# Four graph layers in one kernel: q's bias moved into ScalarE copies, two small products with 64-column weights, and another precomputed order

## The chip, the cores and the metric

The kernel runs on one core of one Trainium2 chip. A core has five engines that run their own instruction queues in order: TensorE (PE in the profile, its weight loads PEld), VectorE (DVE), ScalarE (ACT), GpSimd (POOL) and SyncE (SP), which here issues the DMAs. They wait for each other through semaphores. The metric is the device time of one execution in microseconds (us), taken as the median of several runs; lower is better. One execution was also recorded by the hardware profiler, and its trace is what the views below are read from.

## The reference, cut to what matters

Input x is 128 graphs of 64 nodes with 512 features, adj is 128 matrices of 64 x 64. Four layers follow each other, each of the form x + f(relu(layernorm(x)), adj):

```python
# layer 0: hypergraph convolution twice, H = (adj != 0), w = first row of adj
xw  = h @ W1.T                               # 512 -> 1024
m   = Be * (H.T @ xw);  out = Dn * (H @ m) + b1
z   = layer_norm(relu(out), gamma, beta)
y   = the same convolution of z with W2, b2  # 1024 -> 512
# layer 1: attention from two sums, s = (h @ w) @ a
A   = exp(lrelu(8 * tanh((s_i + s_j) / 8), 0.1)) * adj
out = (A / A.sum(-1) * adj.sum(-1)) @ h @ w
# layer 2: attention with q, k, v
q, k, v = h @ Wq.T + bq, h @ Wk.T + bk, h @ Wv.T + bv
wt  = adj * exp(q @ k.T);  out = (wt / wt.sum(2)) @ v
# layer 3: three-hop diffusion
T   = adj * exp(lrelu(sj + si + ab, 0.2)), rows normalised
out = relu(h @ Wk[0] + bk[0] + T h @ Wk[1] + bk[1] + T T h @ Wk[2] + bk[2])
```

## The kernel before, in words

Tokens are the 128 x 64 nodes; a tile is 128 tokens (two graphs), a group is 4 tiles, and there are 16 groups. A first stage takes every group through layers 0 and 1 and writes x to DRAM (L819); a second stage takes every group through layers 2 and 3 (the loops at the end of the kernel function). Weights stay in SBUF; W1, W2 and w of the first stage are replaced by those of the second. All matmuls are fp32, and each runs as two passes on TensorE, so the trace shows two records for each.

Large products are done with a seven-product scheme over 2 x 2 blocks (`strassen`, L600, for layers 0, 1 and 3; `prod` of layer 2, L851). The common tail is `seven` (L573): three PSUM buffers px, py and pz take the seven products; after four of them ScalarE copies the running sum out into SBUF (`snap`, L581, the copy is L582), and `emit` finishes one of the four output blocks: block (0,0) from py plus the first snapshot, (1,1) from two snapshots, (0,1) from pz plus a snapshot, (1,0) from px. `emit` differs by layer: `biased` (L640) adds a bias row to the snapshot on GpSimd (L646) and the product on VectorE (L648), giving y; `emit_q` (L866) adds q's bias to the snapshot on GpSimd (L876) and the product on VectorE (L877). Block (1,0) has no snapshot, and there ScalarE adds the bias as it copies (L870).

Small products around the change:
- M (L716): per group, four tiles of H^T times (B^-1 H, first column of adj) in one PSUM buffer, 128 columns of weights by 65 moving columns; then two copies of the diagonal blocks (L719). M multiplies h (`left_mul_T`, L547) and finally y (L769).
- T^2 (L968): per group, four tiles of T with T's transpose, 128 by 64; the transposes are VectorE's (L959). T and T^2 multiply h at L984.
- The logits of layer 2 (L889): 32 matmuls with weights of 128 rows by 64 columns, for the two halves of PSUM's partitions in turn.
- L922 multiplies the attention weights with v, which `emit_v` finishes at L912.

The attention sums of layers 1 and 3 need a column of sums spread over all partitions: `across` (L650) writes it to DRAM (L656) and reads it back twice as a row (L660), on SP's queue. Layer 1's rows' denominator (L794) goes the same way. `load_group` (L337) loads a group's adjacency (L339) and x tiles (L345); L790 is the first user of the adjacency in layer 1, L705 to L711 in layer 0.

The order of everything is computed when the kernel is built. Each operation is recorded with an engine, a price in us, and the buffers it reads and writes (`Graph.op`); nothing is issued then. `Graph.run` (L82) plays the operations in time with these prices and with fixed latencies: among those that can start first on an engine it takes the one of lowest priority number, gives out buffers as they come free, and notes the order. The priority of an operation is a running time (`G.prio`), advanced by `step(us)` times STRETCH for the layer and set to group x PERIOD1 or PERIOD2 at each group, plus a shift for the part of the layer it belongs to (`part`, which looks the shift up in the table AT). The instructions are then emitted in that order. Each engine keeps it on the chip, whatever the durations really are.

Where `run` finds TensorE idle for more than 0.5 us, `fill` (L1020) puts matmuls of ones in front of the next product, so many that they take 0.75 of the gap that was computed:

```python
for _ in range(int(gap * FILL / (0.224 if filled else 0.448))):
    nc.tensor.matmul(ps[:, :P], ones, ones, start=True, stop=True)
```

A planned wait thus becomes visible in the code as a number of filler matmuls (L1024), 89 in all in the kernel before.

Of the kernel before, what the change touches and what calls it, by code (L numbers as in the profile page):

```python
# [14 lines left out]
P = 128  # L15
C = 64
# [151 lines left out]
def tile_adj_preln_d4(  # L168
# [82 lines left out]
    def c_mm(n, count):  # L251
        return 2 * count * max(n * 2 / 2400 + 0.0045, 0.1115)

# [20 lines left out]
    def quad(b):  # L274
# [4 lines left out]

    STRETCH, PERIOD1, PERIOD2 = (2.2224, 5.134, 0.2702, 0.07), 81.1, 134.563  # L280
    AT = {
        "x0": -2840.94, "apart": 287.74, "w1": -513.31, "b1": -168.3, "w2": 243.98, "w": 957.54, "c1": 854.05, "l0":
        -2204.52, "c2": 515.04, "l1": 63.21, "c": 117.06, "g0": -3126.92, "g1": -2727.42, "g2": -105.35, "g3":
        -163.16, "g": -95.6, "bq": 1082.42, "l3": 14.31, "wg": 1096.75, "w3": -252.99, "beg0": -102.14, "beg1":
        24.42, "end00": 2.45, "end01": 700.62, "end11": -173.4, "new2": -238.84, "new3": -156.64, "end2": -23.01,
        "end3": -122.96, "load1": -101.64, "load2": 739.49, "m": 1019.23, "h0": -39.7, "p0": 5.17, "z0": -86.76,
        "q0": 9.35, "y0": -36.38, "h1": -35.17, "p1": -35.37, "z1": -20.03, "q1": 2.09, "y1": -79.97, "s": -51.66,
        "t0": 45.29, "e0": -438.27, "t1": -46.02, "e1": -3235.56, "hT": 549.35, "sh": -31.99, "lq": 13.9, "pt":
        -247.06, "v": 437.13, "pv": -1821.4, "s3": -192.56, "tt": -2105.79, "a0": 31.21, "b0": -115.63, "a1": 59.69,
        "b1_": -113.75,  # L290
    }
# [88 lines left out]
    def dot(in0, in1, acc, r, w):  # L380
        j = Buf("o")
        dve(0.77, lambda: nc.vector.scalar_tensor_tensor(j.t, in0(), 1.0, in1(), op0=ALU.mult, op1=ALU.mult,  # L382
                                                         accum_out=acc()), r, [*w, j])
# [129 lines left out]
    def norm_stats(src, k, r):  # L513

        st, mv, rs = Buf("st"), Buf("mv"), Buf("rs")
        for i in range(k):
            dve(0.69, lambda i=i: nc.vector.bn_stats(st.t[:, i, :], src(i)), [r[i]], [(st, i)])  # L517
        dve(0.19, lambda: nc.vector.bn_aggr(mv.t, st.t[:, :k, :].rearrange("p k s -> p (k s)")), [(st, i) for i in range(k)], [mv])  # L518
        pool(0.32, lambda: nc.gpsimd.tensor_scalar_add(rs.t, mv.t[:, 1:2], EPS), [mv], [rs])  # L519
        pool(0.65, lambda: nc.gpsimd.tensor_tensor(rs.t, rs.t, mhalf, ALU.pow), [rs], [rs])  # L520
        return mv, rs

    def offset(mv, rs):
        nm = Buf("nm")
        pool(0.47, lambda: nc.gpsimd.tensor_scalar(nm.t, mv.t[:, 0:1], rs.t, -1.0, op0=ALU.mult, op1=ALU.mult), [mv, rs], [nm])  # L525
        return nm
# [33 lines left out]
    def proj(lhsT, rhs, p, r, first=True, last=True):  # L560
# [6 lines left out]
        pe(c_mm(512, k), mm, r if first else [*r, p], [p])  # L567

    def pv(p):
        t = p[0].t[:, p[1]] if isinstance(p, tuple) else p.t  # L570
        return t.rearrange("p a b -> p (a b)") if len(t.shape) == 3 else t

    def seven(mul, U, n, emit, fifth=None):  # L573

        px, py, pz = (Buf("ps") for _ in range(3))
        fifth = fifth or (U, 0)

        def snap(p, v):  # L581
            act(n / 1200 + 0.17, lambda: nc.scalar.copy(pv(v)[:, :n], p.t[:, :n]), [p], [v])  # L582

        mul[1](px, True)
        snap(px, (U, 0))
        mul[2](py, True)
        emit(0, 0, py, (U, 0), (U, 0))
        mul[6](px, False)
        snap(px, (U, 1))
        mul[5](pz, True)  # L590
        snap(pz, fifth)
        mul[7](px, False)
        snap(px, (U, 2))
        emit(1, 1, fifth, (U, 2), (U, 2))
        mul[3](pz, False)
        emit(0, 1, pz, (U, 1), (U, 1))
        mul[4](px, False)
        emit(1, 0, px, None, (U, 0))

    def strassen(A, keys, B, kc, n, stag, emit):  # L600
# [8 lines left out]
        def comb(d, kd, x_, kx, y_, ky, op):  # L609
            dve(c_v(kc * P), lambda: nc.vector.tensor_tensor(d(), x_(), y_(), op), [*kx, *ky], kd)  # L610

# [28 lines left out]
    def biased(dst, j, p, u, v, row, krow):  # L640
# [3 lines left out]
        if u is not None:  # L644
            (U, iu), iv = u, v[1]
            pool(0.75, lambda: nc.gpsimd.tensor_add(U.t[:, iv], U.t[:, iu], row()[:, cols]), [u, krow], [v])  # L646
            add, ka = (lambda: U.t[:, iv]), v
# [50 lines left out]
    def layer0(g):  # L698
# [15 lines left out]
        def mm():  # L714
            for t in range(T):
                nc.tensor.matmul(pmv()[:, t, :], HT.t[:, t, :], mB.t[:, t, :], start=True, stop=True)  # L716
        pe(c_mm(65, T), mm, [(HT, 0), (HT, C), mB], [pm])
        for s in HALVES:
# [55 lines left out]
    def layer1(g):  # L774
# [26 lines left out]
        for t0 in (0, 2):  # L801
# [4 lines left out]
            def emit_w(i, j, p, u, v, t0=t0):  # L806
                xx, cols = xt[g, t0 + i], slice(j * D // 2, (j + 1) * D // 2)
                if u is not None:
                    U, iu = u
                    pool(0.75, lambda: nc.gpsimd.tensor_add(xx.t[:, cols], xx.t[:, cols], U.t[:, iu]), [xx, u], [xx])  # L810
                dve(c_v(D // 2), lambda: nc.vector.tensor_add(xx.t[:, cols], pv(p)[:, :D // 2], xx.t[:, cols]), [p, xx], [xx])
# [9 lines left out]
    def layer2(g):  # L821
# [14 lines left out]
        for q, (a, ka, b, kb, op) in enumerate((  # L836
# [3 lines left out]
                (lambda: X.t[:, 1], [(X, 1)], lambda: A(0, 1), k[0], ALU.subtract))):  # L840
            dve(c_v(D), lambda q=q, a=a, b=b, op=op: nc.vector.tensor_tensor(X.t[:, q], a(), b(), op), [*ka, *kb], [(X, q)])
        hs = {1: (lambda: A(0, 0), k[0]), 2: (lambda: A(0, 1), k[0]), 3: (lambda: A(1, 1), k[1]), 4: (lambda: X.t[:, 3], [(X, 3)]),
              5: (lambda: X.t[:, 2], [(X, 2)]), 6: (lambda: X.t[:, 1], [(X, 1)]), 7: (lambda: X.t[:, 0], [(X, 0)])}
        pair = lambda f: f.rearrange("p (a n) -> p a n", a=2)

# [20 lines left out]
        def emit_q(i, j, p, u, v):  # L866
# [5 lines left out]
            else:  # L872

                (U, iu), iv = u, v[1]
                at = lambda: pair(U.t[:, iv])
                pool(1.3, lambda: nc.gpsimd.tensor_add(at(), pair(U.t[:, iu]), gb_c[:, 2 * i:2 * i + 2, None].to_broadcast([P, 2, 2 * P])), [u, "gb"], [v])  # L876
                dve(c_v(D), lambda: nc.vector.tensor_add(at(), pair(pv(p)), at()), [p], [v])  # L877
                qs.append((i, j, at, [v]))

        seven({n: prod(WG[n], hs[n], True) for n in range(1, 8)}, Buf("u5"), D, emit_q, Buf("qT"))  # L880

# [22 lines left out]
        def emit_v(i, j, p, u, v):  # L904
# [3 lines left out]
            if u is not None:  # L908
                (U, iu), iv = u, v[1]
                pool(1.3, lambda: nc.gpsimd.tensor_add(pair(U.t[:, iv]), pair(U.t[:, iu]), bias), [u, "bv_b"], [v])  # L910
                add, ka = (lambda: pair(U.t[:, iv])), v
# [20 lines left out]
    def layer3(g):  # L932
# [33 lines left out]
        def m2():  # L966
            for t in range(T):
                nc.tensor.matmul(p2.t[:, t * C:(t + 1) * C], tr.t[:, t, :], tt.t[:, t, 0, :], start=True, stop=True)  # L968
        pe(c_mm(64, T), m2, [*trk, (tt, 2), (tt, 3)], [p2])
        act(0.38, lambda: nc.scalar.copy(tt.t[:, :, 1, :], p2.t[:, :T * C].rearrange("p (t c) -> p t c", t=T)), [p2], [(tt, 1)])  # L970
# [170 lines left out]
```

## Time and profile before

| | us |
|---|---|
| median of 3 runs | 2403.9 |
| lowest and highest run | 2403.34, 2407.2 |
| the profiled execution | 2403.15 |
| span of its instructions | 2400.9 |
| granted TensorE clock, mean | 0.998 |

The prediction is worked out on the profiled execution: what it changes in the span is added to its 2403.15 us, and the median of the runs stands 0.75 us above that.

How to read the views that follow. The page's first part gives an engine's busy time, its share of the span and its instructions. The waits are a list of engine, line and what the instruction at that line waited for, with the total in us, how often, and the longest. A timeline has start, duration, engine, line, operation, written and read tiles, and in brackets the idle time of that engine just before, with what ended it. A tile is named by its buffer; buffers that share memory have a joint name (y_qT holds y in the first stage and q in the second, tmp_mB_s holds M's input among others, bd holds M, T or the attention weights, row_sh holds bias rows or layer 2's X sums). A matmul's recorded duration is modelled and overlaps the next, so its price on TensorE is the distance from its start to the next start: 0.2155 us per pass of 256 moving columns, 0.43 us at 512, 0.112 us for a pass of 128 columns or fewer with 128-column weights. In the groups of instructions, the figures after the bar are busy us, mean ns of one, and idle us before them.

Times by stage, from the stages' busy times: in 300 to 1100 us (first stage) TensorE is busy for 787.27 us of 800, ScalarE for 560.39 and VectorE for 599.55; in 1600 to 2200 us (second stage) TensorE for 594.92 of 600, ScalarE for 320.18 and VectorE for 367.62.

### The profile page before, as it was taken

The page shows a single profiled execution, that of the slowest core. Times are in us where ns is not written, and L with a number is a line of the kernel's source. Part 1 is how long each engine was busy: PE and PEld are TensorE (multiplying, and loading weights), DVE is VectorE, ACT ScalarE, POOL GpSimd, SP SyncE. Part 2 cuts the span into 40 slices and gives each one's busy share as a digit, 9 for nine tenths or more (in the row PEclk, how much of TensorE's full clock was granted, in tenths as well). Part 3 has the DMA queues.
Part 4 walks back from the last instruction along what each step waited for, and adds up shares of the span by engine and source line. Part 5 has one row for each costly group of instructions (what it writes and reads, how often), then busy time and mean ns, then how long its engine had stood idle before and what let it go on. Part 6 is the DMA issues. An engine that isn't in the chain of part 4 may idle for free.

```text
span 2400.9 us, 33897 instructions
## 1 busy us (share of the span) xinstructions
PE 2357.4 (98%) x12022; PEld 1866.8 (78%) x12022; DVE 1636.8 (68%) x3478; ACT 1454.4 (61%) x2226; POOL 976.9 (41%) x1514
## 2 busy tenths in 40 slices
PE   8999999999999999999999999999999999999999
PEld 4676677776767766777788888888888888888888
DVE  7877777777777777777768556474664747557484
ACT  4677676677676676766756456364554546455452
POOL 7244555435555345554344233233323224233241
PEclk9999999999999999999999999999999999999999
DMA  7332222222232322223451423223132231323211
GB/s 263 70 80 57 62 60 72 67 66 54 65 72 66 75 53 62 64 69 71 110 137 40 93 51 73 57 62 84 34 84 56 62 84 29 95 52 69 54 31 42
DMA packets 336920, 171.02 MB, mean 71 GB/s; under 512 B 284656, under 2 KB 290672, under 8 KB 336752
## 3 DMA queue, kind: packets, MB, share of 16 engines
q1 hardware_dynamic: 336752, 168.86, 29.2%
q8 instruction: 95, 1.56, 0.3%
q14 instruction: 73, 0.60, 0.1%
HBM read 66.99 MB, written 34.70 MB: 42 GB/s over the span
## 4 chain that ended last, share of the span: by engine, by line
PE 76%; DVE 10%; DMA 6%; POOL 4%; ACT 2%; issue 1%; SPq 0%; DVEq 0%; ACTq 0%; POOLq 0%
PE ps L618 56%; PE ps L856 8%; PE ps L547 4%; DMA adj<-in_adj_dram 2%; PE ps L769 2%; PE ps L984 2%; PE ps L922 1%; DMA rw<-row 1%; POOL nm L525 1%; POOL rs L520 1%; POOL x L810 1%; DVE st L517 1%; DMA row<-col 1%; DVE x L928 1%; DVE rT_vu_tt L959 1%
## 5 line engine op out<-in xcount | busy, mean ns | idle before, releaser
L582 ACT COPY u<-ps 128x256 f32<-128x256 f32 (+1 forms) x624 | 274.7, 452 | 450.6 <-PE ps L618 279.0
L618 PE MATMUL ps<-wb_mem,s_s_a 128*128 128x256 f32 x2184 | 507.2, 380 | 3.4 <-ACT u L582 3.4
L618 PEld LDWEIGHTS ps<-wb_mem,s_s_a 128*128 128x128 f32 x2184 | 410.8, 190 | 68.2 <-issue 8.5
L538 ACT ACTIVATE h<-x,nm,rs 128x512 f32<-128x512 f32 x384 | 304.7, 813 | 157.4 <-POOL nm L525 142.0
L519 POOL TENSOR_SCALAR rs<-mv 128x1 f32<-128x1 f32 x320 | 108.5, 339 | 458.6 <-DVE mv L518 443.4
L618 PE MATMUL ps<-wb_mem,tmp_mB_s 128*128 128x256 f32 x1152 | 259.8, 380 | 0.7 <-ACT u L582 0.7
L618 PE MATMUL ps<-wa_mem,mT_a 128*128 128x512 f32 x512 | 241.7, 600 | 3.3 <-ACT u L582 3.3
L618 PEld LDWEIGHTS ps<-wb_mem,tmp_mB_s 128*128 128x128 f32 x1152 | 218.1, 190 | 30.9 <-ACT u L582 1.5
L618 PE MATMUL ps<-wb_mem,rT_vu_tt 128*128 128x256 f32 x1024 | 241.2, 379 | 0.5 <-ACT rT_vu_tt L558 0.5
L618 PE MATMUL ps<-wb_mem,mT_a 128*128 128x256 f32 x1016 | 237.8, 379 | 0.0
L618 PEld LDWEIGHTS ps<-wb_mem,rT_vu_tt 128*128 128x128 f32 x1024 | 192.6, 190 | 53.1 <-issue 28.4
L517 DVE BATCH_NORM_STATS2 st<-x 128x6 f32<-128x512 f32 x256 | 174.7, 682 | 66.3 <-DMA x<-xm 52.8
L520 POOL TENSOR_TENSOR rs<-rs,mhalf 128x1 f32<-128x1 f32 x320 | 209.4, 655 | 25.2
L618 PEld LDWEIGHTS ps<-wb_mem,mT_a 128*128 128x128 f32 x1016 | 192.3, 190 | 31.8 <-issue 6.2
L998 POOL TENSOR_TENSOR u<-u,bk_b 128x256 f32<-128x256 f32 x96 | 73.8, 769 | 297.2 <-ACT u L582 297.1
L618 PE MATMUL ps<-wa_mem,s_s_a 128*128 128x512 f32 x384 | 178.2, 594 | 0.0
L618 PEld LDWEIGHTS ps<-wa_mem,mT_a 128*128 128x128 f32 x512 | 96.4, 192 | 100.9 <-issue 92.3
L525 POOL TENSOR_SCALAR nm<-mv,rs 128x1 f32<-128x1 f32 x320 | 146.3, 457 | 31.5
L547 PEld LDWEIGHTS ps<-bd,h 128*128 128x128 f32 x1024 | 131.7, 193 | 31.3 <-issue 13.2
L558 ACT COPY rT_vu_tt<-z_hT 128x1024 uint16<-128x1024 uint16 x128 | 147.0, 1159 | 12.0 <-DMA z_hT<-tmp_mB_s 11.9
L810 POOL TENSOR_TENSOR x<-x,u 128x256 f32<-128x256 f32 x96 | 76.7, 799 | 166.5 <-ACT u L582 166.5
L556 ACT COPY tmp_mB_s<-z_hT 128x1024 uint16<-128x1024 uint16 x128 | 133.7, 1045 | 10.1 <-DVE o L382 5.6
(179 smaller groups left out, 4148.8 us busy)
## 6 DMA issues: line engine op xcount, KB each, us to landing
x<-in_x_dram SPq DMA_DIRECT2D x64, 256.0 KB, 2.7
xm<-x SPq DMA_DIRECT2D x64, 256.0 KB, 2.0
x<-xm SPq DMA_DIRECT2D x64, 256.0 KB, 2.8
out_dram<-x SPq DMA_DIRECT2D x64, 256.0 KB, 2.0
adj<-in_adj_dram SPq DMA_DIRECT2D x32, 256.0 KB, 4.1
rw<-row SPq DMA_DIRECT2D x94, 64.0 KB, 3.2
wb_mem<-in_Wk_dram SPq DMA_DIRECT2D x6, 512.0 KB, 4.8
tmp_mB_s<-in_Wk_dram SPq DMA_DIRECT2D x8, 256.0 KB, 2.9
```

Source lines behind the costliest of these rows:

```text
L517: dve(0.69, lambda i=i: nc.vector.bn_stats(st.t[:, i, :], src(i)), [r[i]], [(st, i)])
L519: pool(0.32, lambda: nc.gpsimd.tensor_scalar_add(rs.t, mv.t[:, 1:2], EPS), [mv], [rs])
L520: pool(0.65, lambda: nc.gpsimd.tensor_tensor(rs.t, rs.t, mhalf, ALU.pow), [rs], [rs])
L525: pool(0.47, lambda: nc.gpsimd.tensor_scalar(nm.t, mv.t[:, 0:1], rs.t, -1.0, op0=ALU.mult, op1=ALU.mult), [mv, rs], [nm])
L538: act(0.82, lambda: nc.scalar.activation(h.t, xx.t, AF.Relu, bias=nm.t, scale=rs.t), [xx, nm, rs], [h])
L547: nc.tensor.matmul(quad(p)[:, c, :], h.t[:, c * P:(c + 1) * P], rhs(), start=True, stop=True)
L556: act(1.05, lambda: nc.scalar.copy(u16(planes.t).rearrange("p (q c) -> p q c", q=2), u16(src()).rearrange("p (c q) -> p q c", q=2)), ksrc, ...
L558: act(1.16, lambda: nc.scalar.copy(u16(dst()).rearrange("p c (k q) -> p c k q", q=2), u16(back()).rearrange("p (q c r) -> p c r q", q=2, c ...
L582: act(n / 1200 + 0.17, lambda: nc.scalar.copy(pv(v)[:, :n], p.t[:, :n]), [p], [v])
L618: nc.tensor.matmul(p.t[:, :n], lhs()[:, c, :], rhs(c), start=first and c == 0, stop=c == kc - 1, skip_group_check=True)
L810: pool(0.75, lambda: nc.gpsimd.tensor_add(xx.t[:, cols], xx.t[:, cols], U.t[:, iu]), [xx, u], [xx])
L856: nc.tensor.matmul(pair(p.t)[:, o, :], a, b, start=first and o == 0 and c == 0, stop=c == 1, skip_group_check=True)
```

## The change

- q's bias: `seven` gets a parameter `biased_by`. With it, the snapshots of the running sums (except the one that goes to `fifth`) are taken by ScalarE in two activations of 256 columns with the bias of their 128 output rows, where there was one copy of 512. `emit_q` then has no addition on GpSimd; VectorE adds the product to the snapshot as before.
- M and T^2: each of the four matmuls with 128-column weights becomes two with 64-column weights, which write the two halves of PSUM's partitions.
- Prices of the planner: TensorE's are lower by about one per cent (256 columns: 0.2138 us per pass where it was 0.2178), M and T^2 are booked at 0.7 us, and some on VectorE and GpSimd are higher.
- STRETCH, PERIOD1, PERIOD2 and all shifts of AT have other values. With the prices they give another order on every engine and queue. The kernel after has 141 filler matmuls.

Lines after the change stand 5 to 8 further down: L716 is L724, L769 is L777, L790 is L798, L794 is L802, L648 is L655, L968 is L974, L922 is L927, L912 is L917, L889 is L894, L856 is L863, L618 is L625.

```diff
     def c_mm(n, count):
-        return 2 * count * max(n * 2 / 2400 + 0.0045, 0.1115)
+        return 2 * count * max(n * 2 / 2412 + 0.0015, 0.1105)
...
-    STRETCH, PERIOD1, PERIOD2 = (2.2224, 5.134, 0.2702, 0.07), 81.1, 134.563
+    STRETCH, PERIOD1, PERIOD2 = (1.8736, 3.1834, 11.5852, 0.0063), 73.347, 141.697
     AT = {
...
     def dot(in0, in1, acc, r, w):
         j = Buf("o")
-        dve(0.77, lambda: nc.vector.scalar_tensor_tensor(j.t, in0(), 1.0, in1(), op0=ALU.mult, op1=ALU.mult,
+        dve(0.81, lambda: nc.vector.scalar_tensor_tensor(j.t, in0(), 1.0, in1(), op0=ALU.mult, op1=ALU.mult,
                                                          accum_out=acc()), r, [*w, j])
...
-    def seven(mul, U, n, emit, fifth=None):
+    def seven(mul, U, n, emit, fifth=None, biased_by=None):
...
-        def snap(p, v):
-            act(n / 1200 + 0.17, lambda: nc.scalar.copy(pv(v)[:, :n], p.t[:, :n]), [p], [v])
+        def snap(p, v, i=None):
+            if biased_by and i is not None:
+                for o in range(2):
+                    act(0.46, lambda o=o: nc.scalar.activation(pair(pv(v))[:, o], pair(p.t)[:, o], AF.Identity, bias=biased_by(i, o)), [p, "gb"], [v])
+            else:
+                act(n / 1200 + 0.17, lambda: nc.scalar.copy(pv(v)[:, :n], p.t[:, :n]), [p], [v])
 
         mul[1](px, True)
-        snap(px, (U, 0))
+        snap(px, (U, 0), 0)
...
-        snap(px, (U, 1))
+        snap(px, (U, 1), 0)
...
-        snap(px, (U, 2))
+        snap(px, (U, 2), 1)
...
         def comb(d, kd, x_, kx, y_, ky, op):
-            dve(c_v(kc * P), lambda: nc.vector.tensor_tensor(d(), x_(), y_(), op), [*kx, *ky], kd)
+            dve(c_v(kc * P) * 1.12, lambda: nc.vector.tensor_tensor(d(), x_(), y_(), op), [*kx, *ky], kd)
...
         def mm():
             for t in range(T):
-                nc.tensor.matmul(pmv()[:, t, :], HT.t[:, t, :], mB.t[:, t, :], start=True, stop=True)
-        pe(c_mm(65, T), mm, [(HT, 0), (HT, C), mB], [pm])
+                for s in HALVES:
+                    nc.tensor.matmul(pmv()[s, t, :], HT.t[:, t, s], mB.t[:, t, :], start=t == 0, stop=True, skip_group_check=True)
+        pe(0.7, mm, [(HT, 0), (HT, C), mB], [pm])
...
                 (U, iu), iv = u, v[1]
-                at = lambda: pair(U.t[:, iv])
-                pool(1.3, lambda: nc.gpsimd.tensor_add(at(), pair(U.t[:, iu]), gb_c[:, 2 * i:2 * i + 2, None].to_broadcast([P, 2, 2 * P])), [u, "gb"], [v])
-                dve(c_v(D), lambda: nc.vector.tensor_add(at(), pair(pv(p)), at()), [p], [v])
+                at = lambda: pair(pv(v))
+                dve(c_v(D), lambda: nc.vector.tensor_add(at(), pair(pv(p)), pair(pv(u))), [p, u], [v])
                 qs.append((i, j, at, [v]))
 
-        seven({n: prod(WG[n], hs[n], True) for n in range(1, 8)}, Buf("u5"), D, emit_q, Buf("qT"))
+        seven({n: prod(WG[n], hs[n], True) for n in range(1, 8)}, Buf("u5"), D, emit_q, Buf("qT"), lambda i, o: gb_c[:, 2 * i + o:2 * i + o + 1])
...
         def m2():
             for t in range(T):
-                nc.tensor.matmul(p2.t[:, t * C:(t + 1) * C], tr.t[:, t, :], tt.t[:, t, 0, :], start=True, stop=True)
-        pe(c_mm(64, T), m2, [*trk, (tt, 2), (tt, 3)], [p2])
+                for s in HALVES:
+                    nc.tensor.matmul(p2.t[s, t * C:(t + 1) * C], tr.t[:, t, s], tt.t[:, t, 0, :], start=t == 0, stop=True, skip_group_check=True)
+        pe(0.7, m2, [*trk, (tt, 2), (tt, 3)], [p2])
```

## The prediction

> **What bounds the kernel now.** I read the page's first part, then the waits of TensorE, then the timeline round the largest of them.
>
> ```profile
> span 2400.9 us, 33897 instructions
> ...
> PE 2357.4 (98%) x12022; PEld 1866.8 (78%) x12022; DVE 1636.8 (68%) x3478; ACT 1454.4 (61%) x2226; POOL 976.9 (41%) x1514
> ```
>
> TensorE is the bound, so only three things count: matmul work, waits, and filler (L1024). The trace's matmul starts, at the median distance of each kind, give 2299 us of useful work, 178 filler passes of 0.112 us (19.8 us), 5 us at both ends, and some 77 us of longer distances: waits, slow-clock stretches in the first 70 us, and changes of tile shape. An edit on another engine is worth only what it takes out of these 77 + 20 us.
>
> ```profile
> PE ps L769 <- DVE y_qT L648: 12.9, 12, 1.6
> PE ps L618 <- ACT u L582: 7.4, 16, 3.1
> PE ps L922 <- DVE rT_vu_tt L912: 4.2, 8, 0.6
> PE ps L968 <- DVE rT_vu_tt L959: 3.4, 7, 1.0
> ```
>
> Columns: total us, times, longest. The first is one wait per group in the first stage (layers 0 and 1, 16 groups of 73.5 us). The third and fourth belong to the second stage (layers 2 and 3, 8 pairs of groups of 145 us). One instance of the first, on three engines:
>
> ```profile
> 290.61 1.89 PE L618 MATMUL ps<-wb_mem,rT_vu_tt 128*128 128x256 f32 x8
> 293.85 1.12 PE L769 MATMUL ps<-y_qT,bd 128*128 128x512 f32 x2 [1.35 <-DVE y_qT L648]
> ...
> 292.71 0.42 DVE L790 TENSOR_REDUCE col<-adj 128x4 f32<-128x256 f32 x1 [2.48 <-DMA adj<-in_adj_dram]
> 293.05 0.41 DVE L648 TENSOR_TENSOR y_qT<-u 128x256 f32<-128x256 f32 x1
> 293.38 0.41 DVE L648 TENSOR_TENSOR y_qT<-ps,u 128x256 f32<-128x256 f32 x1
> ...
> 288.05 0.38 SPq L339 DMA_DIRECT2D adj<-in_adj_dram x1
> ```
>
> The cause is not L648: VectorE stands at L790, which wants the next group's adjacency, issued at 288.05 and landed at 292.7. Both L648 queue behind it.
>
> **What the Trainium skill says.** "TensorE: Matmul & The Clock Gate", Part 1, has VectorE and ScalarE as strict FIFO, and the fence above shows it. The same page, under LDWEIGHTS, times a weight load by its columns, P/1.2 ns (107 ns for 128); here 128-column matmuls with short moving operands start 112 ns apart, so the load is their price. "TensorEngine Tiling (Array Packing)", Key Properties, says that changing the tiling mode drains the engine; the trace puts a number on it below. "ScalarE: Activation LUTs", What ACT_TABLE_LOAD costs, charges some 93 ns more for a per-partition bias; the bias rows below agree roughly (468 ns at 256 columns against 371 ns for a copy).
>
> ```profile
> 278.49 1.00 PE L716 MATMUL ps<-tmp_mB_s,bd 128*128 128x65 f32 x8
> ...
> 1573.84 0.61 PE L1024 MATMUL ps<-ones 128*128 128x128 f32 x4
> 1574.38 1.62 PE L889 MATMUL ps<-u,z_hT 128*64 128x64 f32 x48
> 1575.83 0.64 PE L889 MATMUL ps<-y_qT,z_hT 128*64 128x64 f32 x16
> 1576.39 3.72 PE L856 MATMUL ps<-wa_mem,row_sh 128*128 128x256 f32 x16
> ```
>
> **64-column weights for M and T².** An fp32 matmul is two passes. Now: 8 passes from 278.49 to 279.32, where the next product starts, plus 0.055 us that the next weight load lags: 0.89 us. After: 16 passes of L889's very form. L889's 64 passes take 2.01 us, of which 64 x 0.029 (passes start 58 ns apart by pairs) is 1.86; entry costs 0.09 us (filler's four passes end at 1574.29), the exit 0.15 inside and 0.10 at the next matmul: 0.35 us for both switches. So 16 x 0.029 + 0.35 = 0.82 us, against the 0.70 that the planner now books. Gain 0.07 us x 32 = 2.3 us; bounds: 6.2 us gained at 0.70, some 2 us lost if the switches cost 0.5. As eight of the T² groups end a wait, I take 2.
>
> **q's bias.** Removed: 48 additions on GpSimd (L876, 1122 ns, 53.9 us). Changed: 48 ScalarE copies of 512 columns (L582, 581 ns) become 96 activations of 256, the form of L870:
>
> ```profile
> L870 ACT ACTIVATE y_qT<-ps,gb_c 128x256 f32<-128x256 f32 x32 | 13.4, 468 | 4.2 <-PE ps L856 4.2
> ```
>
> GpSimd loses 53.9 us; ScalarE gains 48 x (2 x 0.468 - 0.581) = 17 us in a stage where it is 53% busy; VectorE's sum (L877, 0.69 us) stays but no longer waits for GpSimd. TensorE waits for none of these now (no L876 or L877 in its waits), so 0, bounds -1 to +4. What is queued behind the longer snaps on ScalarE are layer 3's h tiles; that is reckoned below.
>
> **The new order, first stage.** The instruction lists of both kernels show what moved. T0 is the end of the z product whose evacuation precedes the attention sums. L790 comes equally late after it in both: adjacency issued after the denominator, landed at 292.7 with T0 at 285.44, so T0 + 7.3 here. Before, T0 is followed by four products (1.72 + 3 x 1.73), so L769 is due at T0 + 6.9 and runs at + 8.4. After, one more 512-column product stands ahead of it (1.72 + 1.73 + 1.72 + 1.73 + 1.72): due at T0 + 8.62. VectorE needs, after landing, L790's reduction (0.34 by starts), one aggregation (0.12) and the two sums (0.33 + 0.41): 7.3 + 1.2 = T0 + 8.5. The wait is covered with 0.1 us to spare here. From the measured waits (up to 1.6 us) the landing varies by some 0.5 us, so a rest of 0 to 0.3 us stays in some groups. The next tile's product is due at T0 + 13.0; its chain (0.82 + 1.3 + 0.75 + 0.68 + 0.2 + 0.41 from T0 + 8.5) ends at + 12.7. Tight, but covered. What is now late with L790 is the aggregation of the second z tile, about 3 us later than before; its weights are wanted on TensorE past T0 + 30, and its path (GpSimd 1.4, ScalarE and transposes about 8, sums 3.4) has 10 us of room. Gain: 12.9 less 1.5 = 11.5 us; bounds 0 and 14.
>
> **The new order, second stage.** The new lists put 14 filler passes (before: 4 + 4, pure cost, since no wait follows them) ahead of T² in each pair.
>
> ```profile
> 1582.42 1.10 PE L968 MATMUL ps<-rT_vu_tt,bd 128*128 128x64 f32 x8 [0.45 <-DVE rT_vu_tt L959]
> 1583.42 0.67 PE L922 MATMUL ps<-rT_vu_tt,bd 128*128 128x257 f32 x2
> 1584.65 3.30 PE L922 MATMUL ps<-rT_vu_tt,bd 128*128 128x256 f32 x14 [0.56 <-DVE rT_vu_tt L912]
> ```
>
> From the end of the earlier group's last L922 (1554.40) T² starts 28.0 us later, then 0.99 us of T² and the second wait of 0.8. After: 14 products of 1.73 and L889 (2.2) put T² at + 26.4, with fillers at + 28.0. Its chain: four X sums and an evacuation now stand ahead of three of the four statistics on VectorE (last statistics at + 7.2, not + 3.9); GpSimd's offsets end near + 12.2 (before 9.6); ScalarE's last h near + 13.5; the last dot of the row sum near + 14.2 (before 14.6, since the dots are reordered); row there and back 6.3 as before, + 20.6; then sum and slope to + 22.2; but the exponential now stands behind the logits' first exponential (logits end at + 22.9), so it ends at + 23.9; multiply to transposes, 4.8 us: + 28.7. T² then takes 0.82, and the L922 wait is gone, because the products it follows are 5 us old and not 3.5. Sum 29.5 against 29.8: -0.2 per pair, -1.5 over seven; bounds ±0.8 per pair, so -6 to +6. I take -1.
>
> **Head, turn and end.** Before loses some 22 us in the first 100 (first data at 4.3, slow clock, waits of 1.8, 1.2 and 3.2 us). After loads x first, so the first useful matmul comes near 7 (six more issues of 0.46 us), but M follows sooner and 16 matmuls of filler keep the clock up in a planned gap near 70 us: -3, bounds -8 to +5. Between the stages the planned gaps hold 58 filler matmuls, before 44; at 0.224 us per matmul and a fill of 0.75 that is 17.3 against 13.1 us of gap: +2 after overlap, bounds 0 to +6. The end is alike: 0.
>
> **The sum.** -11.5 - 2 - 1 - 3 + 2 = -15.5 us on a profiled execution of 2403.15 (2.2 us around its span); the median is 0.75 above, so 2403.9 - 15.5, and I say 2388.
>
> **Rivals.** (a) More than that: the exponential is not held, T² starts by + 27.9, and head and M pay fully: -15.5 - 6 - 4 = 2378. For it: the new prices follow the durations measured above; TensorE priced short (0.2138 us a pass of 256 columns; in the trace 0.2155) makes planned gaps smaller in fact. (b) No change: the adjacency lands late by as much again, because VectorE's stall is still there and only its cover moved; the wait stays at 1 us a group: 2402. Against it: the 1.72 us of product is certain. (c) Slower: filler. There are 141 matmuls of it against 89, 52 x 0.223 = 11.6 us. Filler is put in by the planned gap alone; before, the pairs at 1573.84 and 1563.03 were followed by no wait, so they cost their full time. If the planned gaps are mostly absent and half the L769 wait comes back, 11.6 + 6 - 6 - 2 = +9.6: 2413. It decides once more than half of the new filler stands where TensorE had work. For it: the old plan's gaps erred; against it: my walk finds the T² gap at 2.3 us, of which filler takes 1.56. (d) The 64-column form gains nothing: 2390, inside the forecast.
>
> **Chances.** Forecast (with d) 0.58, (a) 0.16, (b) 0.09, (c) 0.17. The likeliest case's own range is 2380 to 2398; the 8-in-10 range leaves out the far ends of (a) and (c): 2375 to 2409. 0.2% (4.8 us) is about what a measurement of this kernel can tell from no change. Faster 0.74, same 0.09, slower 0.17.
>
> **What would show it.** Right: L777 waiting for L655 falls below 4 us in all, first-stage groups at 72.3 us; an M group near 0.82 us; L974 beginning about 0.8 us after its filler, no wait of L927 behind it; pairs at 144.8 us. Wrong: groups still at 73.5, a new wait of over 1 us per group, fillers after which nothing waits, or the first 100 us losing more than 25.

## The result, and the profile after

The changed kernel takes 2387.76 us (median of 3 runs, 2383.98 to 2388.02) against 2403.9 us: ratio 0.9924, 95% interval 0.9902 to 0.9947, 16 us faster. A second comparison (e11 below) gave 2386.01 against 2403.18 us, 0.993 (0.9917 to 0.9944). The prediction was 2388.

The page of the kernel after, its span and first row, in the columns used before:

```profile
span 2386.2 us, 34691 instructions
...
PE 2358.8 (99%) x12382; PEld 1866.0 (78%) x12382; DVE 1613.7 (68%) x3478; ACT 1466.5 (61%) x2274; POOL 906.4 (38%) x1466
```

TensorE is still the bound. Its waits after the change (total us, times, longest):

```profile
PE ps L974 <- DVE rT_vu_tt L964: 7.1, 8, 1.4
...
PE ps L927 <- DVE bd L902: 2.2, 7, 0.3
...
PE ps L625 <- ACT u L589: 2.1, 2, 1.5
...
PE ps L777 <- DVE y_qT L655: 0.8, 3, 0.4
```

The first line of the old list (L769 waiting for y, 12.9 us) is down to 0.8. The second (L618 waiting for ScalarE's snapshot, 7.4 us in 16 instances) is down to 2.1 in two. The wait for T^2's transposes has grown from 3.4 to 7.1 us, and L927 waits for L902, which it did not before.

To place the gain, the matmuls of both traces are laid end to end: each kind of pass counts as useful work with its median distance to the next start (M and T^2 with 0.89 us a group before and 0.81 after, fillers with nothing), and what goes beyond is lost time. Lost time is then read at equal amounts of useful work, so that stages can be compared although the order differs:

| stretch, by useful work done | lost before | lost after | difference | predicted |
|---|---|---|---|---|
| head, 0 to 150 us | 23.3 | 29.9 | +6.6 | -3 |
| first stage, 150 to 1100 us | 21.5 | 4.1 | -17.4 | -11.5 |
| turn, 1100 to 1300 us | 20.3 | 18.4 | -1.9 | +2 |
| second stage and end | 32.7 | 33.1 | +0.4 | -1 |
| work of M and T^2 | | | -2.4 | -2 |
| sum | | | -14.7 | -15.5 |

The spans differ by the same 14.7 us (2400.9 and 2386.2). So the sum was right, but of its terms only the last was. The lost time is read at medians of each kind of pass, so a few tenths of a us in a row mean nothing.

The timeline of the kernel after at the place where the old one waited (start, duration, engine, line, operation, tiles, in brackets the idle time before and its end):

```profile
293.17 0.39 SPq L339 DMA_DIRECT2D adj<-in_adj_dram  x1
...
295.58 1.89 PE L625 MATMUL ps<-wb_mem,s_s_a 128*128 128x256 f32 x8
297.31 1.88 PE L625 MATMUL ps<-wa_mem,mT_a 128*128 128x512 f32 x4
297.34 0.42 DVE L798 TENSOR_REDUCE col<-adj 128x4 f32<-128x256 f32 x1 [1.43 <-DMA adj<-in_adj_dram]
...
297.79 0.37 DVE L655 TENSOR_TENSOR y_qT<-u 128x256 f32<-128x256 f32 x1
298.08 0.42 DVE L655 TENSOR_TENSOR y_qT<-ps,u 128x256 f32<-128x256 f32 x1
...
299.02 1.02 PE L777 MATMUL ps<-y_qT,bd 128*128 128x512 f32 x2
```

VectorE still stands idle for the adjacency (1.43 us here, 23.0 us over 13 groups; before, 33.3 us over 14), but TensorE has the product at 297.31 to do meanwhile. y is ready near 298.5 and L777 is due at 299.02: the stall is not gone, it is covered.

The second stage, same columns:

```profile
1562.89 1.62 DVE L695 TENSOR_TENSOR ee<-rw,col 128x256 f32<-128x256 f32 x1 [4.85 <-DMA rw<-row]
...
1567.63 1.72 PE L1030 MATMUL ps<-ones 128*128 128x128 f32 x14
...
1570.25 0.87 DVE L902 TENSOR_TENSOR bd<-ee,adj 64x256 f32<-64x256 f32 x2
1570.28 0.69 PE L974 MATMUL ps<-rT_vu_tt,bd 128*64 128x64 f32 x16 [0.93 <-DVE rT_vu_tt L964]
...
1571.27 3.93 PE L927 MATMUL ps<-rT_vu_tt,bd 128*128 128x257 f32 x16 [0.31 <-DVE bd L902]
```

T^2 starts 29.0 us after the earlier group's last L927 (1541.24); before it was 28.0 after L922. Fourteen passes of filler and 0.93 us of waiting stand ahead of it, and the attention weights (L902), queued behind the transposes, come 0.31 us late for L927. A pair of groups takes 145.2 us, before 145.1.

### The profile page after: what moved, and what is told of

Its sections match the earlier page's. It is cut to its first block, busy times and chain, and to the rows that moved or that the text cites. A ratio compares the mean times of both kernels' runs of the same rounds, so it can differ in the third digit from the quotient of the medians.

```text
span 2386.2 us, 34691 instructions
## 1 busy us (share of the span) xinstructions
PE 2358.8 (99%) x12382; PEld 1866.0 (78%) x12382; DVE 1613.7 (68%) x3478; ACT 1466.5 (61%) x2274; POOL 906.4 (38%) x1466
## 4 chain that ended last, share of the span: by engine, by line
PE 44%; DVE 4%; DMA 2%; ACT 1%; issue 1%; POOL 0%; SPq 0%; DVEq 0%; ACTq 0%
PE ps L625 26%; PE ps L863 11%; PE ps L990 3%; PE ps L927 2%; DMA rw<-row 1%; DVE o L382 1%; DVE rT_vu_tt L964 1%; DMA row<-col 1%; PE ps L894 1%; ACT h L538 0%; DVE ee L695 0%; PE ps L1030 0%; DVE rT_vu_tt L917 0%; PE ps L547 0%; DVE bd L956 0%
## 5 line engine op out<-in xcount | busy, mean ns | idle before, releaser
L625 PE MATMUL ps<-wb_mem,s_s_a 128*128 128x256 f32 x2184 | 506.8, 380 | 1.5 <-DVE s_s_a L617 0.9
L589 ACT COPY u<-ps 128x256 f32<-128x256 f32 (+1 forms) x576 | 249.2, 441 | 418.4 <-PE ps L625 364.2
L625 PEld LDWEIGHTS ps<-wb_mem,s_s_a 128*128 128x128 f32 x2184 | 411.4, 190 | 70.7 <-issue 13.8
L519 POOL TENSOR_SCALAR rs<-mv 128x1 f32<-128x1 f32 x320 | 98.4, 307 | 484.4 <-DVE mv L518 458.7
L625 PE MATMUL ps<-wb_mem,tmp_mB_s 128*128 128x256 f32 x1152 | 259.8, 380 | 0.0
L625 PEld LDWEIGHTS ps<-wb_mem,tmp_mB_s 128*128 128x128 f32 x1152 | 218.3, 190 | 29.9
L625 PE MATMUL ps<-wa_mem,mT_a 128*128 128x512 f32 x512 | 240.1, 597 | 0.0
L625 PE MATMUL ps<-wb_mem,rT_vu_tt 128*128 128x256 f32 x1024 | 239.9, 379 | 0.0
L625 PE MATMUL ps<-wb_mem,mT_a 128*128 128x256 f32 x1016 | 238.5, 380 | 0.0
L625 PEld LDWEIGHTS ps<-wb_mem,rT_vu_tt 128*128 128x128 f32 x1024 | 193.3, 190 | 52.8 <-issue 25.8
L625 PEld LDWEIGHTS ps<-wb_mem,mT_a 128*128 128x128 f32 x1016 | 191.0, 190 | 31.8 <-issue 4.3
L625 PE MATMUL ps<-wa_mem,s_s_a 128*128 128x512 f32 x384 | 177.9, 600 | 1.6 <-ACT u L589 1.5
L625 PEld LDWEIGHTS ps<-wa_mem,mT_a 128*128 128x128 f32 x512 | 97.5, 191 | 92.8 <-issue 85.1
L547 PEld LDWEIGHTS ps<-bd,h 128*128 128x128 f32 x1024 | 127.5, 192 | 23.4 <-issue 15.0
L525 POOL TENSOR_SCALAR nm<-mv,rs 128x1 f32<-128x1 f32 x320 | 131.6, 411 | 29.8
L556 ACT COPY tmp_mB_s<-z_hT 128x1024 uint16<-128x1024 uint16 x128 | 133.8, 1047 | 9.2 <-PE ps L468 4.1
```

The source lines that it names most:

```text
L519: pool(0.40, lambda: nc.gpsimd.tensor_scalar_add(rs.t, mv.t[:, 1:2], EPS), [mv], [rs])
L525: pool(0.53, lambda: nc.gpsimd.tensor_scalar(nm.t, mv.t[:, 0:1], rs.t, -1.0, op0=ALU.mult, op1=ALU.mult), [mv, rs], [nm])
L547: nc.tensor.matmul(quad(p)[:, c, :], h.t[:, c * P:(c + 1) * P], rhs(), start=True, stop=True)
L556: act(1.05, lambda: nc.scalar.copy(u16(planes.t).rearrange("p (q c) -> p q c", q=2), u16(src()).rearrange("p (c q) -> p q c", q=2)), ksrc, ...
L625: nc.tensor.matmul(p.t[:, :n], lhs()[:, c, :], rhs(c), start=first and c == 0, stop=c == kc - 1, skip_group_check=True)
```

## The experiments

Times in us are against the kernel before on the same chip (2404.57 for e1 to e4, 2397.27 for e5 to e9, 2403.18 for e10 to e12), worked out from the ratio and its interval. The changed kernel's first ratio, put on the scale of e1 to e4, is -18.3 (-23.6 to -12.7); in e11 it stands at -16.8.

| run | what it is | against before |
|---|---|---|
| e1 | after, 128-column M and T^2 | -8.4 (-11.1 to -5.5) |
| e2 | after, q's bias on GpSimd | +8.4 (+5.3 to +11.8) |
| e3 | after, no filler | -1.2 (-3.1 to +0.7) |
| e4 | before, L790 behind L648 | -16.8 (-20.0 to -13.9) |
| e5 | before, q's bias on ScalarE | -1.2 (-3.1 to +1.0) |
| e6 | before, 64-column M and T^2 | -3.6 (-5.5 to -1.4) |
| e7 | e4, e5 and e6 together | -16.5 (-19.4 to -13.4) |
| e9 | e7, no filler from the third pair of groups on | -18.0 (-21.1 to -15.1) |
| e10 | after, L798 behind L655 | -18.7 (-22.1 to -15.6) |
| e11 | after, again | -16.8 (-19.9 to -13.5) |
| e12 | e7, two GpSimd operations swapped | -11.8 (-14.9 to -8.9) |

**e4: is L790 the cause?** Once the order has been computed, one operation is moved back past the two additions:

```diff
         order.sort(key=lambda x: x[:2])
+        for i in [i for i, x in enumerate(order) if x[2].mark == "num"]:
+            nxt = [j for j in range(i + 1, min(i + 60, len(order))) if order[j][2].eng == "DVE"][:2]
+            if all(order[j][2].mark == "y" for j in nxt):
+                order.insert(nxt[-1], order.pop(i))
```

> The kernel before with one edit: in each group of the first stage the reduction of the next adjacency (L790) stands behind the two additions of y (L648) in VectorE's queue, not ahead of them. Theory: L769 waits only because L790 stands ahead of L648 and waits for a DMA; both additions have their inputs 1.5 us earlier, so the wait of L769 for L648 (12.9 us) falls below 1.5 us, groups from 73.5 to 72.5 us, and the time is 12 to 14 us less: 2390 to 2392. The smaller wait of L618 for L582 (0.4 us per group) stays. Rival 1: y's own products are what is late: wait and time stay, 2403. Rival 2: the wait comes back at the next use, since TensorE then reaches L618, L547 or L770's buffers earlier: 2397 or more with a new wait of over 0.5 us per group.

The first TensorE waits of e4 (its lines stand 4 further down than before: L622 is L618, L586 is L582):

```profile
PE ps L622 <- ACT u L586: 7.7, 18, 1.8
PE ps L926 <- DVE rT_vu_tt L916: 4.3, 8, 0.6
PE ps L972 <- DVE rT_vu_tt L963: 3.7, 8, 1.0
```

The wait for y has left the list; the other three of the old list are as they were, within 0.3 us. Lost time in the first stage fell from 21.5 to 5.8 us, and the part of it that stands ahead of y's product from 14.8 us to nothing (the list of waits has 12.9 of these 14.8, and the expectation had counted by the list). The cause is shown: one VectorE instruction that waited for a DMA ahead of two that did not. It is worth 17 us, as much as the whole change, with the old order everywhere else.

**e10: is anything of it left in the new order?** The same move in the changed kernel, past the aggregation and both additions.

> The changed kernel with L798 (the reduction of the next adjacency, L790 before) behind the two additions of y in VectorE's queue. Theory: the new order already covers VectorE's stall with one more product, so little is left to win: the 0.8 us of L777's waits go and nothing else, 0 to 2 us less than the changed kernel on the same chip. Rival: part of the old loss is still there in another place (VectorE still stands idle for 23 us at L798), and 5 us or more come back.

2384.03 against 2386.01 us in e11: 2 us. The product put ahead of L777 had covered nearly all. Two ways to the same 13 to 16 us, and they don't add.

> The changed kernel itself, on the chip of its neighbours here: 0.992 of before again, so that e10 and e12 can be compared with it directly.

**e6 and e1: the 64-column weights in either order.** e6 puts the form into the kernel before, e1 takes it out of the kernel after; the booked prices, and so the order, stay:

```diff
-                for s in HALVES:
-                    nc.tensor.matmul(pmv()[s, t, :], HT.t[:, t, s], mB.t[:, t, :], start=t == 0, stop=True, skip_group_check=True)
+                nc.tensor.matmul(pmv()[:, t, :], HT.t[:, t, :], mB.t[:, t, :], start=True, stop=True)
```

> The kernel before with 64-column weights for M and T^2 and nothing else (still booked at 0.892 us, so the order stays). Theory: 0.81 us a group for 0.89, 32 x 0.08 = 2.6 us less, a bit under that where T^2 is followed by a wait; M's first copy on ScalarE is 0.3 us earlier, but in the old order nothing waits for it: 2 to 3 us less than before. Rival: the 8 us that e1 lost are in the form itself: 6 to 10 us less.

> The changed kernel with M and T^2 in 128-column weights again, everything else and the order as changed (both products are still booked at 0.7 us). Theory: a group of either form costs what its passes and shape switches cost, 0.81 us against 0.89, so 32 x 0.08 = 2.6 us more, or 2.0 where eight T^2 groups hide it behind their wait: 2390. Rival 1: the switches eat the gain: within 0.5 us of 2387.8. Rival 2: the planner's 0.70 us was right and the gain is 6 us: 2394.

In the old order the form is worth 3.6 us, and the 2.6 that were worked out lie in its interval. In the new one its loss costs 8 to 10 us (e1 against the changed kernel, which was not timed on e1's chip), more than the theory and both rivals had. The two profiled executions are only 6.0 us apart: 2.6 us are the work itself (32 x 0.08), 4.2 are new waits in the first stage (lost time there 8.3 us for 4.1), 3.5 are spread over turn and second stage, and the head of e1 loses some 4 us less. e1's list of waits has the new one (its L617 makes sums from mT_a):

```profile
PE ps L625 <- DVE s_s_a L617: 3.5, 11, 0.5
```

One instance of e1, then the same place of the kernel after:

```profile
536.82 1.00 PE L723 MATMUL ps<-tmp_mB_s,bd 128*128 128x65 f32 x8
...
537.86 0.37 ACT L726 COPY bd<-ps 64x256 f32<-64x256 f32 x1 [0.45 <-PE ps L723]
...
538.86 0.37 ACT L726 COPY bd<-ps 64x256 f32<-64x256 f32 x1 [0.64 <-DVE col L731]
539.25 0.59 ACT L549 COPY mT_a<-ps 128x512 f32<-128x512 f32 x1
...
540.86 2.41 PE L625 MATMUL ps<-wa_mem,s_s_a 128*128 128x512 f32 x5 [0.37 <-DVE s_s_a L617]
```

```profile
539.11 0.69 PE L724 MATMUL ps<-tmp_mB_s,bd 128*64 128x65 f32 x16
...
539.84 0.37 ACT L727 COPY bd<-ps 64x256 f32<-64x256 f32 x1 [0.17 <-PE ps L724]
...
540.85 0.37 ACT L727 COPY bd<-ps 64x256 f32<-64x256 f32 x1 [0.64 <-DVE col L732]
541.24 0.59 ACT L549 COPY mT_a<-ps 128x512 f32<-128x512 f32 x1
...
542.45 4.13 PE L625 MATMUL ps<-wa_mem,s_s_a 128*128 128x512 f32 x9
```

M's first copy starts 0.73 us after M in the narrow form and 1.04 after in the wide one. In the new order ScalarE has L549 behind M's second copy, and the product after the next needs what L549 makes: the 0.31 us come out on TensorE as 0.37. So in the first stage the form pays by its result being early, and not by the 0.08 us of TensorE alone; what it is worth elsewhere in the new order is not shown.

**e5 and e2: q's bias in either order.** e5 has the bias in the snapshots with the old order kept (the additions keep their price in the plan but issue nothing); e2 puts the additions back into the new one, each right behind its copy (`biased_by` is then the addition itself):

```diff
-                for o in range(2):
-                    act(0.46, lambda o=o: nc.scalar.activation(pair(pv(v))[:, o], pair(p.t)[:, o], AF.Identity, bias=biased_by(i, o)), [p, "gb"], [v])
+                act(0.46, lambda: nc.scalar.copy(pv(v)[:, :n], p.t[:, :n]), [p, "gb"], [v])
+                act(0.46, lambda: biased_by(i, pair(pv(v))), [p, "gb"], [v])
...
-        seven({n: prod(WG[n], hs[n], True) for n in range(1, 8)}, Buf("u5"), D, emit_q, Buf("qT"), lambda i, o: gb_c[:, 2 * i + o:2 * i + o + 1])
+        seven({n: prod(WG[n], hs[n], True) for n in range(1, 8)}, Buf("u5"), D, emit_q, Buf("qT"), lambda i, f: nc.gpsimd.tensor_add(f, f, gb_c[:, 2 * i:2 * i + 2, None].to_broadcast([P, 2, 2 * P])))
```

> The kernel before with q's bias in ScalarE's snapshots and nothing else: the planner's prices and the order of every engine stay as before, the 48 additions on GpSimd are gone. Theory: in the old order no wait of TensorE ends on that addition, so the edit by itself is worth nothing: within 2 us of before. That e2 lost 25 us would then belong to the new order, which was planned without the addition. Rival: the addition is on the path of q in any order, and the edit alone gains 5 us or more.

> The changed kernel with q's bias back on GpSimd: one ScalarE copy of 512 columns and one GpSimd addition for each of the 48 snapshots, at the same place in the order. Theory: nothing on TensorE waits for it, so within 1 us of 2387.8, and no wait of TensorE for L884 or for GpSimd. Rival: the new order leans on the shorter path (no 1.12 us of GpSimd between copy and sum), so PSUM or q comes late in each of 16 groups: 3 us or more on top, 2391 or more.

Nothing in the old order, 25 us in the new one, all of it in the second stage: its pairs take 147.6 to 149.5 us instead of 145.2. The lists of waits, for e2 three lines of TensorE and ScalarE's for GpSimd's offsets, then the latter of the kernel after:

```profile
PE ps L974 <- DVE rT_vu_tt L964: 14.7, 8, 2.1
PE ps L863 <- ACT u L586: 4.2, 7, 0.7
...
PE ps L863 <- ACT u L589: 3.6, 6, 0.6
```

```profile
ACT h L538 <- POOL nm L525: 99.5, 75, 2.8
```

```profile
ACT h L538 <- POOL nm L525: 60.8, 54, 2.8
```

The additions (58.7 us on GpSimd in e2) stand in a queue with the offsets of layer 3's rows; h comes later, and T^2's wait doubles. That is a third of the loss. ScalarE takes snapshots (L586, L589) behind the late h, and L863 waits for them, which it doesn't in the kernel after. By the distances in the second stage L863 loses 10.2 us more than there, T^2 7.6 and L927 6.6; of the last, some 4.6 (an estimate from passes at twice their distance) are three falls of TensorE's clock (see e3). e2 is not how the old form would do in an order planned for it: it shows that the new order leans on the additions' absence.

**e3 and e9: what is a filler worth?** e3 is the changed kernel with `FILL = 0.0`. e9 is e7 (described below) with the filler left out after the first 16 filled gaps (`FIRST`), which takes away the last 12, from the third pair of groups on:

```diff
-        for _ in range(int(gap * FILL / (0.224 if filled else 0.448))):
+        n = int(gap * FILL / (0.224 if filled else 0.448))
+        for _ in range(n if len(filled) < FIRST else 0):
```

> The changed kernel without any filler matmul, same order. Theory: a filler followed by a wait costs nothing, one followed by none costs its time. In the trace five fillers of the turn (16, 16, 14, 18 and 30 passes, 10.5 us) are followed by no wait, the others are: so 6 to 10 us less, 2378 to 2382, all of it between 1140 and 1280 us, and the wait of L974 grows by 1.6 us per pair while the pairs stay at 145.2 us. Rival 1: the waits that the fillers stand for come back elsewhere in the turn: within 2 us of 2387.8. Rival 2: TensorE's clock falls in the waits that are now empty: 2392 or more, with a lower granted clock.

> As e7, without the filler of the second stage (the 4 + 4 passes per pair of groups, of which the first four are followed by no wait and the last four by one of 0.09 us). Theory, from e3: the fillers stand over waits of about their own length, and a wait without them is at least as long: within 2 us of e7, and the waits of L860 and L893 grow by 0.4 us each per pair. Rival, as the prediction has it: they are pure cost, since nothing waits after them: 6 to 7 us less than e7, 2377.

Without filler the changed kernel is some 16 us slower, not 6 to 10 faster: the second rival of e3 was right. Lost time rose by 3 us in the head, 6.6 in the turn and 10.6 in the second stage. In the turn each of the five fillers that no wait had followed (1.78, 1.78, 1.56, 2.01 and 3.35 us) gives way to lost time of about its own length (2.24, 1.58, 1.73, 1.58 and 3.59 us): there were waits under all of them, 10.7 us for 10.5. What the turn lost beyond that is for the greater part the clock, which stands at 0.50 in 1169.2 to 1172.6, 1261.4 to 1268.2 and 1288.7 to 1292.1 us of e3; the passes that start at twice their usual distance there put it at 5.2 of the 6.6 us (an estimate). In the second stage it is the clock: L927 loses 11.4 us more by the distances, and nothing else does. One pair of e3, TensorE's timeline, and then a table in steps of 2 us (stretch, length, busy time and instructions of five engines, granted clock, DMA share, GB/s):

```profile
1576.44 1.89 PE L863 MATMUL ps<-wa_mem,z_hT 128*128 128x256 f32 x8
1580.83 0.69 PE L974 MATMUL ps<-rT_vu_tt,bd 128*64 128x64 f32 x16 [2.50 <-DVE rT_vu_tt L964]
1581.82 5.48 PE L927 MATMUL ps<-rT_vu_tt,bd 128*128 128x257 f32 x16 [0.31 <-DVE bd L902]
```

```profile
1578.83:1580.83 2.00, 0.00 (x1) 0.00 (x1) 1.89 (x8) 0.51 (x1) 0.00 (x0) 1.00 0.68 129
1580.83:1582.83 2.00, 1.69 (x19) 1.22 (x20) 1.94 (x4) 0.37 (x1) 0.00 (x0) 0.84 0.01 2
1582.83:1584.83 2.00, 2.00 (x6) 1.54 (x6) 0.98 (x4) 0.00 (x0) 0.10 (x1) 0.50 0.00 0
1584.83:1586.83 2.00, 2.00 (x9) 1.68 (x8) 1.93 (x7) 0.00 (x0) 0.00 (x0) 0.80 0.00 0
```

After 2.5 us without a matmul the clock falls to 0.50 soon after work has begun again, and L927 takes 5.48 us instead of 3.93: 1.5 us for each pair. The Trainium skill, "TensorE: Matmul & The Clock Gate", Part 1, has the clock halved after an idle window of about 3.4 us; here about 2.5 us were enough (2.6 to 3.1 us from the last matmul's start to T^2's), in each of the eight pairs (146.4 to 147.8 us apart). Whether T^2's short passes and the 0.31 us behind them count with the wait, no run separates. With filler the clock stays at 1.00 there, although 1.2 us between the last filler's start and T^2's are still empty.

The length of the wait does not decide it alone. In e2 six pairs have 2.2 to 2.3 us from the last filler's start to T^2's, and the clock fell after three of them; in e1 it fell once after 1.6 us (filler at 1572.25, T^2 at 1573.86, clock 0.50 from 1576.40 to 1578.40), and not after the same 1.6 us at 1281.45. What else decides stays open.

e9 shows another kind of filler. The short ones that no wait followed had none under them: without them the lost time at their place falls from 0.44 to 0.00 us ahead of L868 and from 0.54 to 0.09 ahead of L901 (L856 and L889 before), 4.9 us in all. It comes back a few products later, 3.6 us at L868 and 1.7 at T^2 (L981, 1.6 us in e7's list):

```profile
PE ps L981 <- DVE rT_vu_tt L971: 3.0, 7, 1.0
PE ps L868 <- ACT u L592: 2.8, 7, 0.6
```

So the gain that the rival promised (6 to 7 us) did not come, but the theory had the waits in the wrong place. In time e9 and e7 are 1.5 us apart, with overlapping intervals.

**e7: do the parts add?** The old order, L790 moved, the bias and the weights as in the change.

> The kernel before with three edits and its own order: L790 behind L648 (as in e4), q's bias on ScalarE (as in e5), 64-column weights (as in e6). Theory: they add up, e4's 17 us and 2 to 3 us for the weights and about nothing for the bias: 2383 to 2385, 3 us faster than the changed kernel with its new order. Rival: with L769's wait gone another wait takes up what the weights free: 2387.

-16.5 us, where e4 alone had -16.8 on another chip; the forecast sum of 19 to 20 us lies at the end of e7's interval or beyond. There may be less to win on e7's chip: the wait for y is 10.1 us in both e5 and e6, not 12.9. That the parts add is not shown; what is shown is that three small edits on the old order win as much as the changed kernel does.

**e12: one more wait, a miss.** Where `nm` (L529 in e7) stands directly ahead of an addition of layer 1 on GpSimd, the addition goes first:

```diff
+        for i in [i for i, x in enumerate(order) if x[2].mark == "nm"]:
+            nxt = [j for j in range(i + 1, min(i + 60, len(order))) if order[j][2].eng == "POOL"][:1]
+            users = [j for j in range(i + 1, min(i + 60, len(order))) if order[j][2] in order[i][2].succ]
+            if nxt and order[nxt[0]][2].mark == "xu" and all(j > nxt[0] for j in users):
+                order.insert(nxt[0], order.pop(i))
```

> e7 with one more swap, on GpSimd: where L529 (a row's offset) stands directly ahead of L822 (x plus the snapshot in layer 1), L822 goes first. In e7's trace the snapshot that the next product waits for (0.39 us per group, L629 waiting for ScalarE's L588) waits for VectorE's L823, that for L822 at 600.50 us, and L822 for L524 and L529 ahead of it. Theory: L822 starts 0.3 us earlier, the wait of L629 shrinks from 0.4 to 0.1 us per group: 3 to 5 us less than e7, 0.991 of before and faster than the changed kernel. Rival: L529 is then late for the h that ScalarE makes from it, and the wait moves there: no gain.

```profile
PE ps L634 <- ACT u L593: 5.6, 6, 2.2
...
PE ps L556 <- ACT h L547: 2.7, 13, 0.3
```

The wait for the snapshot went in most groups (17 instances to 6), but L556 now waits for h 13 times (by the distances it loses 9.9 us more there than in e7), and the first stage loses 14.8 us instead of 5.4; e12 is 4.4 us slower than the changed kernel on the same chip (e11). The rival was right: the offset was as urgent as the addition. No version beat the changed kernel by more than the 2 us of e10, whose runs (2382.2 to 2386.4) overlap those of e11 (2384.7 to 2387.7).

## Why the prediction was right, and where it was not

- **First-stage wait (-11.5): right in its mechanism, too small.** The distances ahead of L769 and L777 account for 14.8 us of lost time before and 1.3 after, -13.5; the list of waits alone has -12.1, near the -11.5 and inside the bounds of 0 and 14. The predicted spare time of 0.1 us, with landings that vary by 0.5, is 0.5 us in the instance above, and three groups still wait; e4 and e10 show the cause and the cover. A group takes 71.9 us (the median distance of M's starts), predicted 72.3, before 73.6. Of the 5.9 us that the term lacks, 2 are its own and 3.5 are the second line of the prediction's own list of waits, L618 waiting for L582: it was printed and never priced. It was 0.4 us in each of 11 groups behind L547, because the snapshot's only buffer waited for an addition of layer 1 on VectorE; the new order loses 0.75 us there for 4.3. e4 still has that wait, since its order is the old one (its L815 is L811, its L586 L582):

```profile
604.74 1.47 DVE L815 TENSOR_TENSOR x<-u,x 128x256 f32<-128x256 f32 x1 [0.62 <-POOL x L814]
...
606.25 0.37 ACT L586 COPY u<-ps 128x256 f32<-128x256 f32 x1 [1.81 <-DVE x L815]
...
606.67 1.99 PE L622 MATMUL ps<-wb_mem,s_s_a 128*128 128x256 f32 x8 [0.23 <-ACT u L586]
```

- **64-column weights (-2): right for the old order, too small for the new one.** The group takes 0.81 us, predicted 0.82; e6 agrees with the sum. What was left out is that M's result comes 0.31 us earlier, on a path where the new order has no room (e1).
- **q's bias (0): right for the edit alone (e5).** But the prediction priced it as if it could be added to an order; e2 shows that the order depends on it. ScalarE's busy time rose by 12 us, not by the 17 that were reckoned.
- **Second stage (-1): wrong sign, small.** The residual wait after the filler is 0.9 us for 0.8. The row landed at +21.65 us and not at +20.6, so T^2 came at +29.0 for +28.7; that the exponential would be held by ScalarE was wrong (it ran at once, at 1565.00). "No wait of L927 behind it" failed: 0.3 us for L902. Together 30.0 us against the predicted 29.5 and 29.8 before; pairs at 145.2, not 144.8. (29.5 for 29.8 is -0.3 per pair, where the prediction wrote -0.2.)
- **Head (-3): wrong, outside its bounds.** It lost 6.6 us more. The first useful matmul came at 9.0 us, not near 7, since the x tiles are loaded ahead of what L468 needs; and in the stretch where the new order builds up its pipeline 32 filler passes, which the prediction put near 70 us, and 1.06 us of waiting (135.72 to 140.35) stand ahead of an L625 that needs sums of a z tile whose transposes by DMA landed late. One execution says little of a head, but seven traces with the old order lose 17.9 to 23.3 us up to 150 us of work (21.4 in the mean), five with the new one (e3 left out) 26.1 to 29.9 (27.9). The prediction's own sign of being wrong, over 25 us lost in the first 100, came up: 25.1.
- **Turn (+2): wrong sign.** It lost 1.9 us less. The planned gaps were counted as cost beyond the old ones, but 15.1 us of filler and waits behind it became 16.3, and the other lost time fell from 5.2 to 2.1 us.
- **Rivals.** (c), filler as pure cost, is refuted for the new order: its large fillers stand over waits of about their length and keep the clock up (e3). That no wait follows a filler was the prediction's sign for cost, and it is no such sign: it was seen five times in the turn. Of the old 4 + 4 passes the prediction said "pure cost, since no wait follows them"; they had no wait under them, but what they took is lost at later waits without them (e9). (b) fell with the wait. (a) did not come: the exponential ran at once, but T^2 did not start by +27.9, and the head lost time. (d) is refuted by e1 and e6.

So the largest term was right in its cause, and that the time would fall by such an amount was no accident. That it came within 1 us of 2388 was luck: the head's error (+9.6 us) and the second stage's (+1.4) were met by those of the first stage (-5.9) and the turn (-3.9).

## What to carry to other kernels

When an engine with an in-order queue shows a wait, look for what stands ahead of the named instruction: here one reduction that waited for a DMA cost as much as a whole new order won, and moving it by two places was enough. A filler that no wait follows may still be exactly as long as the wait under it, and may hold the clock up; take it out before calling it a cost. Price every line of the list of waits that is printed, and price an edit in the order that it will run in: taking the 64-column weights and the moved bias out of the order that was planned with them cost 8 to 10 and 25 us, where putting them into the old order won 3.6 and about 1.

## What the runs showed of the hardware

- A wait of some 2.5 us without a matmul was enough for TensorE's clock to fall to half in eight of eight pairs of e3, and shorter ones (2.2 us in e2, 1.6 in e1) were at times. It falls late: in e3 T^2's passes at 1580.83 still run at full speed, and those of L927 start 0.43 us apart, not 0.215, from 1583.0 to 1585.6.
- A product in 64-column weights delivers earlier than its share of TensorE tells: the first copy of M starts 0.73 us after M's start in 13 of the 16 groups, with 128-column weights (e1) 1.04 in 14 of them.
- The same transfers landed at different times on different chips: with the old order the adjacency took 4.0 us from issue to landing (median) in e4 and in e12, on two chips, and 3.7 to 3.8 in the four traces of the chip of e5, where the wait that hangs on it is 10.1 us (e5, e6) and not the 12.9 of the trace before.
